# A two-layer graph and expert network on one core: row additions leave GpSimd, norms share instructions, and the last sixteen batches start three expert pairs in a period

## The chip, the cores and the metric

The kernel runs on one core of a Trainium2 chip. The metric is the device time of one execution in microseconds. Before the change it is 1796.04 us, the median of three runs (1791.09, 1796.04 and 1798.93 us). A difference of about 0.5% is the least that such runs can tell from no change.

The core has five engines with a queue of instructions each: TensorE (PE in the profile, its weight loads apart as PEld), VectorE (DVE), ScalarE (ACT), GpSimd (POOL) and SyncE (SP), which here only starts transfers. An engine works through its own queue in order, so an instruction that waits holds up all that stand behind it.

## The reference

64 batches of 256 rows by 256 columns pass two layers. All batches share one 256 x 256 neighbour matrix. What counts for this change is the number of norms (four for each batch), the two residual additions, and the routing of each row to two of eight experts:

```python
# layer 0 (adj_ffn)
x = x + _L0_gnn_ref(_layernorm(x, axis=-1), adj, L0_gnn_W, L0_gnn_a)   # 4 heads, softmax over neighbours, ELU
x = x + _L0_ffn_ref(_layernorm(x, axis=-1), L0_ffn_weight, L0_ffn_bias)  # x @ W.T + bias
# layer 1 (adj_ffn)
x = x + _L1_gnn_ref(_layernorm(x, axis=-1), adj, L1_gnn_W, L1_gnn_a)   # 1 head, ReLU
x = x + _L1_ffn_ref(_layernorm(x, axis=-1), router_w, w1, b1, w2, b2)

def _moe(tokens, router_w, w1, b1, w2, b2):      # the last of the four
    probs = softmax(tokens @ router_w.T)
    rw, re = top_k(probs, 2)                     # two experts for each row
    rw = rw / rw.sum(-1)
    out = tokens
    for e in range(8):
        h = gelu(tokens @ w1[e] + b1[e])
        out = out + combine[:, e:e+1] * (h @ w2[e] + b2[e])
```

## The kernel before

**Tiles and jobs.** A batch is a tile of 128 partitions x 2 x 256 numbers. The program is unrolled in Python. Every batch is a generator (`batch_layers`, from line 373) that emits some instructions, yields a rank, and goes on when it is next called. The loop at the end of the kernel function (lines 895 to 925) counts steps. In a step each live generator is called once, in the order of its last rank, lowest first, so the order of instructions on every engine is written by this loop and not by a planner. Three steps are a period (`TICKS = 3`), and a new batch begins in the first step of each period (phase 0). A batch lives for about 18 steps, so six batches are in work at once, three steps apart.

**The norms.** `norm_stats` (line 287) lets VectorE gather mean and variance (`bn_stats`, `bn_aggr`, lines 290 and 291), and GpSimd then makes 1/sqrt(variance + eps) in two instructions, an addition (line 293) and a power (line 294), over two numbers for each partition. A batch has four norms. By the order of the steps, the norm of one batch's input and that of another's first residual fall in phase 0 of every period; the norm before layer 1's attention and the one before the experts, again of two different batches, fall in phase 1. `rstd`, the result, is first used a step or more later: as the scale in ScalarE's exponentials (line 323) and VectorE's product (line 327) of `projected`, in VectorE's residual (line 414), and in `by` (lines 440 and 443).

**The two additions.** GpSimd adds the bias row to the first residual (`x1b`, line 401, in phase 0) and the ReLU result to the second (`x2`, line 434, in phase 0). Both work on 128 x 512 numbers.

**The experts.** Batches are routed in chunks: twelve of 4 batches, six of 2 and two of 1. The last two batches (`dense`) run through all eight experts instead. After a chunk's routing on VectorE (`top_two`, `route`, `allot`), GpSimd sends every row to its two places in a table in DRAM (`send`, line 741: 16 indirect transfers for a chunk of 4 batches). A send is emitted two at a time, in the steps of phase 1 and 2 only: `later` (line 752) yields again in phase 0. A pair of tiles (256 rows of one expert) is the unit of expert work (`expert_pair`): SyncE loads the pair (`xr`, line 599), the next step loads the expert's weights (`we`, line 610), the next transposes on TensorE (`px`, line 617), the next does the first product (`ph`, line 649), and after that come the second (`py`, line 664), VectorE's bias addition into `y` (line 670), ScalarE's scaling of `y` (line 642), and at last `scatter` (line 681), in which GpSimd starts two indirect transfers that add the 256 rows to the output. The rows of two pairs may meet, so the transfers of a pair wait for both of the pair before. One pair is scattered in a step.

**How pairs begin.** In phase 2 of each period a credit grows by 2 (by 3 when no batch is left to begin) up to 3, and each waiting pair that begins takes 1:

```python
if phase == 2:
    credit = min(credit + (2.0 if more else 3.0), 3.0)
    while waiting and credit >= 1.0:
        credit -= 1.0
        begin(waiting.pop(0)(), 90)
```

A chunk of 4 batches brings 8 pairs at once, so with an empty list behind it the credit has grown to 3, and four periods begin 3, 2, 2 and 1 pairs. 131 pairs are begun in all, 14 of them at the very end for the partly filled tiles. There are six buffers for `y`, five for `xr`, seven for `we`. The two dense batches bring 16 further jobs of the same kind, without sends and scatters, two in a period at the end; their results take `y` buffers too. The output of the last dense batch is stored behind the last scatter.

Of the kernel before, what the change touches and what calls it, by code (L numbers as in the profile page):

```python
# [26 lines left out]
def kernel(  # L27
# [17 lines left out]
    nc = tc.nc  # L45
    B, N, D = x.shape
# [4 lines left out]
    NT = N // P  # L51
    EPS = 1e-5
# [6 lines left out]
    CHUNKS = (4,) * 12 + (2,) * 6 + (1, 1)  # L59
# [9 lines left out]
    TICKS = 3  # L69

    const = ctx.enter_context(tc.tile_pool(name="const", bufs=1))
    io = ctx.enter_context(tc.tile_pool(name="io", bufs=2))
    work = ctx.enter_context(tc.tile_pool(name="work", bufs=2))
# [33 lines left out]
    nc.vector.memset(ones, 1.0)  # L107
    mean_w = const.tile([P, P], F32, tag="mean_w", name="mean_w")
    nc.vector.memset(mean_w, 1.0 / D)
    mhalf = const.tile([P, NT], F32, tag="mhalf", name="mhalf")  # L110
    nc.vector.memset(mhalf, -0.5)

    adj_i = work.tile([P, NT, N], adj.dtype, tag="z", name="adj_i", bufs=6)
# [25 lines left out]
    def gnn_weights(w, a, heads, slope, name):  # L139

        d = D // heads
        wx = const.tile([P, KT, heads, d + 3], F32, tag=name, name=name)
        for k in range(KT):
            nc.sync.dma_start(
                out=wx[:, k, :, :d],  # L150
                in_=w[k * P : (k + 1) * P, :].rearrange("p (h d) -> p h d", h=heads),
            )
        av = work.tile([P, 2, d], F32, tag="e", name=name + "_a")
        nc.scalar.dma_start(out=av.rearrange("p s d -> p (s d)"), in_=rows_to_all(a, 2 * d))
        prod = work.tile([P, heads, d], F32, tag="hp", name=name + "_p")
        for k in range(KT):
            for s, c in ((0, d + 1), (1, d)):
                nc.vector.tensor_mul(
                    prod, wx[:, k, :, :d], av[:, s : s + 1, :].to_broadcast([P, heads, d])
                )  # L160
                nc.vector.tensor_reduce(wx[:, k, :, c : c + 1], prod, AX.X, ALU.add)
            nc.vector.tensor_scalar(
                wx[:, k, :, d + 1 : d + 2], wx[:, k, :, d + 1 : d + 2], 1.0 - slope, None,
                op0=ALU.mult,
            )
            nc.vector.tensor_scalar(
                wx[:, k, :, d + 2 : d + 3], wx[:, k, :, d : d + 1], slope - 1.0, None,
                op0=ALU.mult,
            )
        flat = wx.rearrange("p k h c -> p k (h c)")  # L170
        center(flat, heads * (d + 3))
        return flat
# [29 lines left out]


    C_B1, WROW = KT * D, KT * D + 64
    WBUFS, XBUFS = 7, 5
    wpack = tc.dram_tile([E, P, WROW], F32, name="wpack")
    w2s = const.tile([P, E, KT * D], F32, tag="w2s", name="w2s")
    b2s = const.tile([P, E, D], F32, tag="b2s", name="b2s")
# [74 lines left out]

    def norm_stats(src):
        stats = small.tile([P, NT, 6], F32, tag="stats", name="stats")
        mv = small.tile([P, NT, 2], F32, tag="mv", name="mv", bufs=6)
        for t in range(NT):
            nc.vector.bn_stats(stats[:, t, :], src[:, t, :])  # L290
            nc.vector.bn_aggr(mv[:, t, :], stats[:, t, :])  # L291
        rstd = small.tile([P, NT], F32, tag="rstd", name="rstd", bufs=8)
        nc.gpsimd.tensor_scalar_add(rstd, mv[:, :, 1], EPS)  # L293
        nc.gpsimd.tensor_tensor(rstd, rstd, mhalf, ALU.pow)  # L294
        return mv, rstd

    def transposed(src, tag="xT", bufs=4):
        pt = bank("pt", [KT, N])
# [71 lines left out]
    def batch_layers(b, c0, xng, lg):  # L370
# [4 lines left out]
        _, rstd = norm_stats(x0)  # L375
# [14 lines left out]
                rinv[:, t, :, None].to_broadcast([P, H, HD]), ALU.mult,  # L390
            )
        yield 20
        ex = work.tile([P, NT, D], F32, tag="e", name="e")
        nc.scalar.activation(ex, hp, AF.Exp)

        x1 = work.tile([P, NT, D], F32, tag="x1", name="x1", bufs=2)
        nc.vector.scalar_tensor_tensor(x1, hp, 0.0, x0, op0=ALU.max, op1=ALU.add)
        nc.vector.scalar_tensor_tensor(x1, ex, 1.0, x1, op0=ALU.min, op1=ALU.add)
        yield 30
        x1b = work.tile([P, NT, D], F32, tag="x1b", name="x1b")  # L400
        nc.gpsimd.tensor_add(x1b, x1, bias_f[:, None, :].to_broadcast([P, NT, D]))
        _, rstd = norm_stats(x1)
        xT = transposed(x1)
        yield 70
# [25 lines left out]
        for t, pv in enumerate(pvs):  # L430
            nc.scalar.activation(  # L431
                rel[:, t, :], pv[:, 0, :D], AF.Relu, scale=rinv[:, t, :]
            )
        nc.gpsimd.tensor_add(x2, x2, rel)  # L434
        yield 60
        mv, rstd = norm_stats(x2)
        yield 15

# [221 lines left out]
    def result(hT, e):  # L660
        py = bank("py", [2, D])
        for t in range(2):
            for f in range(KT):
                nc.tensor.matmul(  # L664
                    py[:, t, :], hT[:, f, t * P : (t + 1) * P],
                    w2s[:, e, f * D : (f + 1) * D].rearrange("p e c -> p (e c)"),
                    start=(f == 0), stop=(f == KT - 1),
                )
        y = io.tile([P, 2, D], F32, tag="y", name="y", bufs=6)
        nc.vector.tensor_add(y, py, b2s[:, e, :].to_broadcast([P, 2, D]))  # L670
        return y

# [76 lines left out]
        sent.append(d.ins.name)  # L749
        nc.gpsimd.nop()  # L750

    def later(rank):

        yield rank
        while (len(order_steps) - 1) % TICKS == 0:
            yield rank

    def route(c, row0, nt, n, last, xng, lg):
# [3 lines left out]
        ohs, first, ed = top_two(c, nt, lg)  # L762
        m = rt([E, nt], "m")
        tt(m.rearrange("p e t -> p t e"), ohs[0], ohs[1], ALU.add)
        yield from later(75)

        mf = m.rearrange("p e t -> p (e t)")
        pp = bank("pp", [2, E, nt])
# [26 lines left out]
            vec.tensor_reduce(posf[:, k], ohs[k], AX.X, ALU.add)  # L795
        pos = rt([2, nt], "pos", 4, I32)
        vec.tensor_copy(pos, posf)
        yield from later(75)
        r4 = rt([nt, 4], "r4")
        vec.tensor_scalar(r4[:, :, 0:1], token[:, :nt, None], float(row0), None, op0=ALU.add)  # L800
        vec.tensor_scalar(r4[:, :, 1:2], first[:, :, None], float(E), None, op0=ALU.add)
# [7 lines left out]
        if last:  # L809
            tt(at, at, run[:, :, nt - 1], ALU.add)  # L810
            ends_at = rt([E], "ends_at", 2, I32)
            vec.tensor_copy(ends_at, at)
        yield from later(95)
        mark = len(sent)
        for t in range(nt):
            for k in range(2):
                send(xng[t // NT][:, t % NT, :], pos[:, k, t : t + 1])
            if not last:
                yield from later(95)
            elif t % 2:  # L820
                yield 95
        needs = sent[mark:]
# [72 lines left out]
    batches = jobs()  # L895
    step, more, credit = 0, True, 0.0
    SETUP_AT = 4
    with tc.manual_schedule():
        while more or active or waiting or dense_jobs or scatters:
            phase = step % TICKS  # L900
            if phase == 0 and more:
                nxt = next(batches, None)
                more = nxt is not None
                if more:
                    begin(nxt, 40)
            if step >= SETUP_AT and setup:
                begin(setup.pop(0)(), 90)
            if phase == 2:
                credit = min(credit + (2.0 if more else 3.0), 3.0)
                while waiting and credit >= 1.0:  # L910
                    credit -= 1.0
                    begin(waiting.pop(0)(), 90)
                for _ in range(2):
                    if dense_jobs:
                        begin(dense_jobs.pop(0)(), 90)
            if scatters:
                def one():
                    scatter()
                    return
                    yield  # L920
                begin(one(), 97)
            order_steps.append(step)
            for entry in sorted(active, key=lambda a: a[:2]):
                entry[0] = next(entry[2], None)
            active[:] = [a for a in active if a[0] is not None]
            step += 1

# [34 lines left out]
```

## Time and profile before

| | us |
|---|---|
| median of three runs | 1796.04 |
| the profiled execution's own time | 1822.89 |
| its span, from the first instruction to the last | 1821.2 |
| TensorE matmuls busy | 1629.5 (89%) |
| TensorE weight loads busy | 1433.0 (79%) |
| VectorE busy | 1231.4 (68%) |
| GpSimd busy | 1084.2 (60%) |
| ScalarE busy | 839.9 (46%) |
| mean granted TensorE clock | 0.937 of full speed |

The profiled execution is 1.5% longer than the median of the runs. Durations are its own. The page gives for each engine the busy time and its share of the span, then the span in 40 slices, then groups of instructions by line, with the mean of one and the idle time before them. Other views list who waited for whom, instructions in order of time, and the busy times in a stretch. Weight loads overlap matmuls, so the two rows of TensorE are not to be added. An indirect transfer's busy time on GpSimd is that of making its descriptors, not of the transfer.

### The profile page before, as it was taken

The page shows a single profiled execution, that of the slowest core. Times are in us where ns is not written, and L with a number is a line of the kernel's source. Part 1 is how long each engine was busy: PE and PEld are TensorE (multiplying, and loading weights), DVE is VectorE, ACT ScalarE, POOL GpSimd, SP SyncE. Part 2 cuts the span into 40 slices and gives each one's busy share as a digit, 9 for nine tenths or more (in the row PEclk, how much of TensorE's full clock was granted, in tenths as well). Part 3 has the DMA queues.
Part 4 walks back from the last instruction along what each step waited for, and adds up shares of the span by engine and source line. Part 5 has one row for each costly group of instructions (what it writes and reads, how often), then busy time and mean ns, then how long its engine had stood idle before and what let it go on. Part 6 is the DMA issues. An engine that isn't in the chain of part 4 may idle for free. (4 is left out here: it accounts for less than half of the span.)

```text
span 1821.2 us, 30155 instructions
## 1 busy us (share of the span) xinstructions
PE 1629.5 (89%) x9254; PEld 1433.0 (79%) x9254; DVE 1231.4 (68%) x4680; ACT 839.9 (46%) x1773; POOL 1084.2 (60%) x1164
## 2 busy tenths in 40 slices
PE   6998889899999999999999999999989998778692
PEld 5787778788888888888878788887878887667582
DVE  6889887867685858686766768688678876522231
ACT  1243333355554555554545545555455545443241
POOL 1333645557575767767676757576685767644444
PEclk9999989899998999998989999999899989889897
DMA  4410211235344444544354534444353436576663
GB/s 137 140 36 24 71 60 53 79 109 121 105 95 104 109 126 108 132 103 110 93 119 112 119 91 95 118 111 128 84 127 101 107 82 166 118 186 139 135 139 43
DMA packets 137374, 192.90 MB, mean 106 GB/s; under 512 B 18680, under 2 KB 91392, under 8 KB 137216
## 3 DMA queue, kind: packets, MB, share of 16 engines
q1 hardware_dynamic: 86592, 122.61, 22.0%
q0 software_dynamic: 49632, 67.39, 20.6%
q8 instruction: 76, 1.25, 0.3%
q10 hardware_dynamic: 992, 0.99, 0.2%
q14 instruction: 82, 0.67, 0.1%
HBM read 101.77 MB, written 89.15 MB: 105 GB/s over the span
## 5 line engine op out<-in xcount | busy, mean ns | idle before, releaser
L681 POOL DMA_INDIRECT out_dram<-y,to x262 | 419.4, 1601 | 231.1 <-DMA out_dram<-y,to 103.5
L360 PE MATMUL pv<-q,z 128*128 128x65 f32 (+1 forms) x2560 | 394.4, 314 | 5.3 <-DVE z L346 5.0
L360 PEld LDWEIGHTS pv<-q,z 128*128 128x128 f32 x2560 | 364.9, 210 | 21.1 <-DVE z L346 5.4
L293 POOL TENSOR_SCALAR rstd<-mv 128x2 f32<-128x2 f32 x256 | 81.2, 317 | 376.2 <-DVE mv L291 355.6
L741 POOL DMA_INDIRECT xs<-xng,pos x248 | 261.2, 1053 | 68.2 <-issue 66.0
L315 PE MATMUL pq<-wx,xT 128*128 128x268 f32 (+1 forms) x1024 | 265.4, 402 | 35.8 <-ACT xT L305 31.8
L649 PE MATMUL ph<-sT,we 128*128 128x256 f32 x1048 | 252.6, 397 | 48.1 <-ACT sT L621 22.9
L346 DVE SCALAR_TENSOR_TENSOR z<-pd,q,mask 128x256 f32<-128x256 f32 x640 | 265.1, 473 | 9.9 <-PE pd L339 7.5
L649 PEld LDWEIGHTS ph<-sT,we 128*128 128x128 f32 x1048 | 205.0, 200 | 80.6 <-ACT sT L621 29.4
L664 PE MATMUL py<-w2s,hT 128*128 (+1 forms) x1176 | 265.4, 381 | 0.6 <-ACT hT L655 0.6
L315 PEld LDWEIGHTS pq<-wx,xT 128*128 128x128 f32 x1024 | 188.1, 194 | 85.8 <-ACT xT L305 50.6
L664 PEld LDWEIGHTS py<-w2s,hT 128*128 128x128 f32 x1176 | 220.5, 191 | 29.3 <-ACT hT L655 1.0
L305 ACT COPY xT<-pt 128x512 f32<-128x512 f32 x256 | 144.9, 589 | 192.8 <-PE pt L301 127.6
L327 DVE SCALAR_TENSOR_TENSOR q<-pq,rstd,q 128x256 f32<-128x256 f32 x256 | 112.4, 479 | 154.5 <-ACT q L323 150.7
L655 ACT ACTIVATE hT<-ph,we 128x256 f32<-128x256 f32 x294 | 123.3, 471 | 173.4 <-PE ph L649 122.9
L670 DVE TENSOR_TENSOR y<-py,b2s 128x512 f32<-128x512 f32 x147 | 96.7, 688 | 149.2 <-PE py L664 77.9
L294 POOL TENSOR_TENSOR rstd<-rstd,mhalf 128x2 f32<-128x2 f32 x256 | 184.2, 719 | 21.4
L642 ACT ACTIVATE y<-y,w 128x256 f32<-128x256 f32 x262 | 112.9, 498 | 177.5 <-DVE y L670 171.1
L290 DVE BATCH_NORM_STATS2 stats<-x 128x6 f32<-128x256 f32 x384 | 155.9, 406 | 0.0
L408 PE MATMUL pf<-wfT,xT 128*128 128x256 f32 x512 | 145.7, 435 | 0.1
L323 ACT ACTIVATE q<-pq,rstd 128x12 f32<-128x12 f32 (+1 forms) x256 | 56.5, 265 | 162.3 <-POOL rstd L294 150.8
L434 POOL TENSOR_TENSOR x<-x,rel 128x512 f32<-128x512 f32 x64 | 109.2, 1706 | 25.2 <-ACT rel L431 25.0
(147 smaller groups left out, 2259.2 us busy)
## 6 DMA issues: line engine op xcount, KB each, us to landing
we<-wpack SPq DMA_DIRECT2D x147, 288.0 KB
xr<-xs SPq DMA_DIRECT2D x131, 260.0 KB
xin<-in_x_dram SPq DMA_DIRECT2D x64, 256.0 KB
out_dram<-base SPq DMA_DIRECT2D x64, 256.0 KB
out_dram<-y,to POOLq DMA_INDIRECT x262
xs<-xng,pos POOLq DMA_INDIRECT x248
xs<-fill SPq DMA_DIRECT2D x9, 260.0 KB
wpack<-wt SPq DMA_DIRECT2D x8, 288.0 KB
```

The lines of the kernel that those rows point to most:

```text
L290: nc.vector.bn_stats(stats[:, t, :], src[:, t, :])
L294: nc.gpsimd.tensor_tensor(rstd, rstd, mhalf, ALU.pow)
L305: nc.scalar.copy(dst, pt)
L315: nc.tensor.matmul(pq.rearrange("p h c -> p (h c)"), xT[:, k, t * P : (t + 1) * P], wx[:, k, :], start=(k == 0), stop=(k == KT - 1),)
L346: nc.vector.scalar_tensor_tensor(z[:, j, :], pd[:, i, :], q[:, j, h, d + 2 : d + 3], mask[:, j, :], op0=ALU.max, op1=ALU.mult,)
L360: nc.tensor.matmul(pv[:, h, :], z[:, j, t * P : (t + 1) * P], q[:, j, h, : d + 1], start=(j == 0), stop=(j == NT - 1),)
L408: nc.tensor.matmul(pf[:, t, :], xT[:, k, t * P : (t + 1) * P], wfT[:, k, :], start=(k == 0), stop=(k == KT - 1),)
L649: nc.tensor.matmul(ph[:, f, :], we[:, k * D + f * P : k * D + (f + 1) * P], xT[:, k, :], start=(k == 0), stop=(k == KT - 1),)
L655: nc.scalar.activation(hT[:, f, :], ph[:, f, :], AF.Gelu, bias=we[:, C_B1 + f : C_B1 + f + 1])
L664: nc.tensor.matmul(py[:, t, :], hT[:, f, t * P : (t + 1) * P], w2s[:, e, f * D : (f + 1) * D].rearrange("p e c -> p (e c)"), start=(f == 0 ...
L681: d = nc.gpsimd.indirect_dma_start(out=out_rows, out_offset=bass.IndirectOffsetOnAxis(ap=to[:, t : t + 1], axis=0), in_=y[:, t, :], in_off ...
L741: d = nc.gpsimd.indirect_dma_start(out=xs_d[: E * CAP * PAIR, :], out_offset=bass.IndirectOffsetOnAxis(ap=at, axis=0), in_=xe, in_offset=None,
```

## The change

GpSimd's two additions go to VectorE: the one for `x1b` stands right after `x1`, a step earlier than before, and the one for `x2` a step later than before, ahead of the statistics that read it. Two norms of a step share one addition and one power over four numbers; when a step has a single norm, the loop finishes it after all other work of that step. From batch 48 on (step 144) the credit grows by 3. The last four routed chunks also send in phase 0. `y` has eight buffers, and the ELU's exponential `e` one instead of two.

```diff
-    mhalf = const.tile([P, NT], F32, tag="mhalf", name="mhalf")
+    mhalf = const.tile([P, 2 * NT], F32, tag="mhalf", name="mhalf")
...
-    WBUFS, XBUFS = 7, 5
+    WBUFS, XBUFS, YBUFS = 7, 5, 8
...
+    half_done = []
+
     def norm_stats(src):
         stats = small.tile([P, NT, 6], F32, tag="stats", name="stats")
-        mv = small.tile([P, NT, 2], F32, tag="mv", name="mv", bufs=6)
+        if half_done:
+            mv, rstd = half_done[0]
+            at = NT
+        else:
+            mv = small.tile([P, 2 * NT, 2], F32, tag="mv", name="mv", bufs=4)
+            rstd = small.tile([P, 2 * NT], F32, tag="rstd", name="rstd", bufs=5)
+            half_done.append((mv, rstd))
+            at = 0
         for t in range(NT):
             nc.vector.bn_stats(stats[:, t, :], src[:, t, :])
-            nc.vector.bn_aggr(mv[:, t, :], stats[:, t, :])
-        rstd = small.tile([P, NT], F32, tag="rstd", name="rstd", bufs=8)
-        nc.gpsimd.tensor_scalar_add(rstd, mv[:, :, 1], EPS)
-        nc.gpsimd.tensor_tensor(rstd, rstd, mhalf, ALU.pow)
-        return mv, rstd
+            nc.vector.bn_aggr(mv[:, at + t, :], stats[:, t, :])
+        if at:
+            finish_norms(2 * NT)
+        return mv[:, at : at + NT, :], rstd[:, at : at + NT]
+
+    def finish_norms(n):
+        mv, rstd = half_done.pop()
+        nc.gpsimd.tensor_scalar_add(rstd[:, :n], mv[:, :n, 1], EPS)
+        nc.gpsimd.tensor_tensor(rstd[:, :n], rstd[:, :n], mhalf[:, :n], ALU.pow)
...
-        ex = work.tile([P, NT, D], F32, tag="e", name="e")
+        ex = work.tile([P, NT, D], F32, tag="e", name="e", bufs=1)
...
+        x1b = work.tile([P, NT, D], F32, tag="x1b", name="x1b")
+        nc.vector.tensor_add(x1b, x1, bias_f[:, None, :].to_broadcast([P, NT, D]))
         yield 30
-        x1b = work.tile([P, NT, D], F32, tag="x1b", name="x1b")
-        nc.gpsimd.tensor_add(x1b, x1, bias_f[:, None, :].to_broadcast([P, NT, D]))
         _, rstd = norm_stats(x1)
...
-        nc.gpsimd.tensor_add(x2, x2, rel)
         yield 60
+        nc.vector.tensor_add(x2, x2, rel)
         mv, rstd = norm_stats(x2)
...
-        y = io.tile([P, 2, D], F32, tag="y", name="y", bufs=6)
+        y = io.tile([P, 2, D], F32, tag="y", name="y", bufs=YBUFS)
...
-    def later(rank):
+    def later(rank, c):
         yield rank
-        while (len(order_steps) - 1) % TICKS == 0:
+        while (len(order_steps) - 1) % TICKS == 0 and c < len(CHUNKS) - 4:
             yield rank
...
+    DRAIN_AT = TICKS * (B - 16)
...
-                credit = min(credit + (2.0 if more else 3.0), 3.0)
+                credit = min(credit + (2.0 if step < DRAIN_AT else 3.0), 3.0)
...
             for entry in sorted(active, key=lambda a: a[:2]):
                 entry[0] = next(entry[2], None)
+            if half_done:
+                finish_norms(NT)
```

More of the change, by code (lines that the diff above doesn't have):

```diff
@@ L152, in gnn_weights @@
             )
-        av = work.tile([P, 2, d], F32, tag="e", name=name + "_a")
+        av = work.tile([P, 2, d], F32, tag="e", name=name + "_a", bufs=1)
         nc.scalar.dma_start(out=av.rearrange("p s d -> p (s d)"), in_=rows_to_all(a, 2 * d))
@@ L764, in route @@
         tt(m.rearrange("p e t -> p t e"), ohs[0], ohs[1], ALU.add)
-        yield from later(75)
+        yield from later(75, c)
         mf = m.rearrange("p e t -> p (e t)")
@@ L797, in route @@
         vec.tensor_copy(pos, posf)
-        yield from later(75)
+        yield from later(75, c)
         r4 = rt([nt, 4], "r4")
@@ L812, in route @@
             vec.tensor_copy(ends_at, at)
-        yield from later(95)
+        yield from later(95, c)
         mark = len(sent)
@@ L818, in route @@
             if not last:
-                yield from later(95)
+                yield from later(95, c)
             elif t % 2:
```

## The prediction

> **What bounds the kernel now.** I read the page first, then the busy times by stretch, the instructions around one stall, and the end.
>
> ```profile
> PE 1629.5 (89%) x9254; PEld 1433.0 (79%) x9254; DVE 1231.4 (68%) x4680; ACT 839.9 (46%) x1773; POOL 1084.2 (60%) x1164
> PEclk9999989899998999998989999999899989889897
> ```
>
> TensorE is nearly full, but its clock falls again and again (granted 0.937 on average). To see why, I cut the middle into periods, from one batch's first transpose to the next. A chunk of four batches repeats periods of about 24.4, 23.0, 21.3 and 31 us. The long one is the period in which three pairs were begun at once. Two of these, with busy time and count of PE, PEld, DVE, ACT and POOL in turn, then clock, DMA share and GB/s:
>
> ```profile
> 739.50:765.40 25.90, 23.39 (x144) 20.52 (x143) 15.89 (x55) 14.65 (x29) 20.76 (x22) 1.00 0.64 160
> 834.10:865.10 31.00, 28.29 (x144) 25.07 (x143) 16.05 (x55) 14.66 (x29) 21.36 (x22) 0.83 0.55 143
> ```
>
> The same 144 matmuls take 25.9 us at full clock and 31.0 us at 0.83: half speed for some 10 us. What precedes it shows at 450 us in the order of time, here on POOL, ACT, DVE, POOL, SP and PE in turn:
>
> ```profile
> 427.18 1.84 POOL L401 TENSOR_TENSOR x1b<-x,bias_f 128x512 f32<-128x512 f32 x1
> 428.42 0.79 POOL L293 TENSOR_SCALAR rstd<-mv 128x2 f32<-128x2 f32 x1
> ...
> 430.30 0.71 POOL L294 TENSOR_TENSOR rstd<-rstd,mhalf 128x2 f32<-128x2 f32 x1
> 431.04 0.43 ACT L323 ACTIVATE q<-pq,rstd 128x12 f32<-128x12 f32 x2 [1.63 <-POOL rstd L294]
> 431.35 0.88 DVE L327 SCALAR_TENSOR_TENSOR q<-pq,rstd,q 128x256 f32<-128x256 f32 x2 [2.30 <-ACT q L323]
> ...
> 436.50 0.22 POOL L293 TENSOR_SCALAR rstd<-mv 128x2 f32<-128x2 f32 x1 [0.75 <-DVE mv L291]
> ...
> 439.09 1.26 POOL L741 DMA_INDIRECT xs<-xng,pos  x1 [0.30 <-issue]
> 442.73 2.93 SPq L599 DMA_DIRECT2D xr<-xs  x3
> 448.85 0.63 PE L617 MATMUL px<-ident,xr 128*128 128x128 f32 x4 [1.88 <-DMA xr<-xs]
> 449.31 6.28 PE L360 MATMUL pv<-q,z 128*128 128x65 f32 x32
> ```
>
> This is one chain. GpSimd finishes a scatter at 426.49, then does two additions and two norms until 431.0; ScalarE waits for the second norm, VectorE waits for ScalarE, and from there VectorE runs without a pause to the statistics of phase 1, behind which stand that phase's norm and two sends. SyncE's load of pairs waits for the send before it (545.2 us of such waits in its own view, 33 of them). With two pairs the data are in time; with three the third is 1.88 us late, the clock falls to 0.5 from 450.0 to 460.3, and the next 32 matmuls take 6.28 us where 3.80 us is usual.
>
> At the end TensorE is no longer the bound:
>
> ```profile
> 1804.95 1.55 POOL L681 DMA_INDIRECT out_dram<-y,to  x1 [3.04 <-DMA out_dram<-y,to]
> 1806.81 1.55 POOL L681 DMA_INDIRECT out_dram<-y,to  x1 [0.30 <-issue]
> 1811.22 1.55 POOL L681 DMA_INDIRECT out_dram<-y,to  x1 [2.86 <-DMA out_dram<-y,to]
> ```
>
> Each pair's scatter waits for the one before to land, at least some 6.4 us from pair to pair (1804.95 to 1811.22 is 6.27). The last 29 pairs start from 1615.70 to 1811.22, 6.98 us each.
>
> **The change part by part**, against the profiled execution of 1822.9 us (span 1821.2); the runs' median is 0.985 of it, and the result is scaled by that.
>
> *Additions and norms.* GpSimd loses two additions of 1.70 us a batch (109.2 and 108.1 us in 64). In a stall's chain they take 2.5 us, since they overlap a little. Four norms of 0.317 + 0.719 us become two. A power over four numbers is not in the trace; it lies between 0.71 us (two numbers cost no more than the fixed part) and 1.22 us (the 0.5 us by which power exceeds the addition's 0.21 us is all per number). I take 1.0, the middle, as no row is nearer. At 450 us the shared norm then starts when the last statistics are in, 426.94, and ends at 428.3 instead of 431.0. VectorE's 2.30 us wait goes, as its work before it (line 346) ends at 429.05. VectorE gains two additions of 0.69 us (line 398 does 128x512 with both inputs in SBUF in 0.692). The one for x2 lies in this very chain, ahead of the statistics, and costs 0.69; the one for x1b lies in phase 2, in idle time before the next waits. The longer power costs the sends 0.3. Sends and loads move forward by 2.3 - 0.7 - 0.3 = 1.3 us. The scatter in between starts no earlier than its predecessor's landing (about 429.4), and at its 3.5 us ends before the new norm. The stall of 1.88 us shrinks to about 0.6, and the other seven chunks look alike (VectorE waits 2.65 to 4.06 us at this place, TensorE 1.46 to 2.5).
>
> Here a rule and a row differ. "TensorE: Matmul & The Clock Gate" of the Trainium skill (Part 1) has the clock fall after an idle window of about 3.4 us. By it no gap here is long enough, and eight stalls are worth 8 x 1.3 = 10 us. In this trace gaps of 1.82 to 2.5 us were followed by 6.8 or 10.2 us at half clock seven times out of seven, and one of 1.46 us was not. I go by the rows. The seven long periods exceed 25.9 us by 5.0, 4.8, 4.0, 5.1, 5.5, 5.9 and 3.6 us, 33.9 together; with the 10 of the stalls that is 44, and I take **-40**, one chunk keeping its stall. Between the ends: 0 if the loads come no earlier, -50 if the stalls vanish.
>
> A second rule speaks against moving the additions. "SBUF — State Buffer" (Who interferes with whom) says that a VectorE instruction with two SBUF inputs shuts out a GpSimd instruction that reads SBUF. The trace agrees: the norm's addition takes 0.21 us, or 0.79 at 428.42. By the rule 128 moved additions could each hold GpSimd for 0.6 us, 77 us in all. But the one for x2 precedes the statistics that its norm waits for, and that for x1b meets sends; I count nothing, and 0.6 us on the path wherever they do meet.
>
> *VectorE's own limit.* Around 1251 to 1276 and 1355 to 1390 us, where two-batch chunks are routed, VectorE hardly pauses. There its 1.38 us a period has no cover: six such periods, **+8**. GpSimd waits for it there up to 9.4 us, and TensorE behind that.
>
> *Single norms* occur at the start and for the last batches; then the norm stands behind that step's scatter (up to 4 us of waiting for its predecessor). What is late is VectorE's residual or `by` in the next step. For some four norms with half of it on the path: **+4** (0 to 16).
>
> *Three pairs a period.* Following the loop step by step, the last scatter comes four steps sooner (237 steps become 233), and by step 208, when the last batches end, 107 pairs are scattered instead of 102. Five pairs move into the full part. On TensorE a pair is 1.87 + 1.78 + 0.44 us (a third of `ph` x24 5.60 and of `py` x24 5.34, and `px` x4): 4.1 us, so **+20** if TensorE is full there, +5 if they fall into the pauses of 5.6 and 6.3 us around 1551 and 1573. I take 20. Each brings its loads on SyncE's queue (260 and 288 KB) and two scatters of 1.85 us each on GpSimd, which has just been relieved of more. Seven more periods start with three loads; if two keep a stall long enough for the clock, at 5 us each, **+10** (0 to 42).
>
> *The tail.* Five pairs fewer: 5 x 6.98 = **-35**. Eight `y` buffers: VectorE waited for one 10 times, 48.5 us in all, and behind it a store and weight loads queued on SyncE, until TensorE stood for 15 us at 1692. The 28 steps of 6.98 us are 16 us over 6.4; half of that, **-8** (0 to -16). `e` with one buffer: its next writing comes a period after its reading, nothing. Sends in phase 0 let the last chunks' pairs wait in the list sooner, where five already wait: nothing.
>
> Sum: -40 + 8 + 4 + 20 + 10 - 35 - 8 = -41, so 1782 us, and times 0.985 **1755 us**.
>
> **The rivals.**
>
> (1) *The loads come no earlier*, since another wait (a scatter, the added VectorE work, the longer power) takes the place of the rstd wait, or the plain runs, 27 us faster than the profiled one, have few half-clock stretches to lose. Then the first term is 0: -1 us, **1795 us**. For it: GpSimd idles 0.75 us ahead of phase 1's norm, so it is not itself what is short there. Against it: VectorE's wait for rstd stands in all eight chains.
>
> (2) *Slower: the third load is late in every period.* If stalls stay and each of the seven added three-load periods gets one, the terms are 0 and +42: 0 + 8 + 4 + 20 + 42 - 35 - 8 = +31, **1826 us**. It decides from a third load about 1.5 us late on, the longest gap that left the clock alone. For it: VectorE is fuller in this stretch. Against it: the same relief acts there.
>
> (3) *More gain*: the five pairs fill pauses (+5), no added stall, full relief in the tail: -40 + 8 + 4 + 5 + 0 - 35 - 16 = -74, **1722 us**.
>
> **How the numbers follow.** Forecast 0.56, rival 1 0.16, rival 2 0.10, rival 3 0.18. The forecast alone spans 1738 to 1778. For 8 in 10 the range reaches over rival 1 and most of rival 3: 1715 to 1799. The measurement can tell about 0.5%, 9 us: rival 1 gives most of its chance to "within", a little to either side. Faster 0.80, same 0.10, slower 0.10.
>
> **What would show it.** Right: VectorE's wait before line 327 (2.3 us and more) gone; third transposes under 1 us late; three-pair periods of 25 to 26 us and clock slices without the regular dips; 24 instead of 29 pairs in the tail at 6.4 to 7 us. Wrong: half-clock stretches after 1070 us more frequent than before; GpSimd's norms waiting longer for VectorE's statistics; pairs in the tail at 7 us or more in spite of the buffers.

## The result, and the profile after

After the change the kernel takes 1766.45 us (median of four runs, 1762.49 to 1771.64), against 1793.64 us for the kernel before (four runs, 1791.09 to 1798.93): a ratio of 0.985, 95% interval 0.981 to 0.989. It is faster by 27 us. The forecast of 1755 us is 11 us, or 0.6%, too low; its direction and range held.

The profiled execution after took 1769.78 us (span 1768.1). That is 53 us below the profiled execution before, twice what the runs show, because the one profiled before had lost the clock more often than most (it stood 1.5% above its median). A second profile of the kernel before, span 1801.2 us, is therefore used beside the first.

Page of the kernel after, busy times and granted clock in 40 slices:

```profile
PE 1594.2 (90%) x9254; PEld 1401.9 (79%) x9254; DVE 1297.7 (73%) x4808; ACT 827.5 (47%) x1767; POOL 840.5 (48%) x788
PEclk9999899999999999899999999898998999898997
```

GpSimd has lost 244 us of busy time and VectorE has gained 66. The same 9254 matmuls are busy 35 us less. Of the first 25 slices of the clock two are at 8 tenths, against five in before's first profile; from slice 26 on the dips remain.

Windows of the kernel after, two of the periods in which three pairs begin (busy time and count of PE, PEld, DVE, ACT and POOL, then clock, DMA share and GB/s):

```profile
541.70:566.50 24.80, 23.31 (x144) 20.56 (x143) 18.01 (x59) 15.29 (x31) 16.63 (x15) 1.00 0.62 162
728.30:759.70 31.40, 28.66 (x145) 25.14 (x144) 18.38 (x59) 15.57 (x31) 17.42 (x16) 0.84 0.54 139
```

Between batches 20 and 48 seven such periods take 24.3 to 24.8 us, but for one of 31.3 us. In the first profile of before they take 25.9 to 31.8, in the second 25.2 to 32.8; the sums are 212, 201 and 179 us. This is the chain of the prediction in the kernel after, in order of time, at the same chunk (DVE, POOL, SP, PE, ACT and DVE in turn):

```profile
438.47 0.88 DVE L341 SCALAR_TENSOR_TENSOR q<-pq,rstd,q 128x256 f32<-128x256 f32 x2 [0.55 <-ACT q L337]
440.54 0.68 DVE L449 TENSOR_TENSOR x<-x,rel 128x512 f32<-128x512 f32 x1
444.35 0.23 POOL L308 TENSOR_SCALAR rstd<-mv 128x4 f32<-128x4 f32 x1 [1.70 <-DVE mv L301]
444.67 1.04 POOL L309 TENSOR_TENSOR rstd<-rstd,mhalf 128x4 f32<-128x4 f32 x1
447.31 0.98 POOL L755 DMA_INDIRECT xs<-xng,pos  x1 [0.30 <-issue]
450.29 1.50 SPq L613 DMA_DIRECT2D xr<-xs  x3
455.51 0.63 PE L631 MATMUL px<-ident,xr 128*128 128x128 f32 x4 [0.28 <-DMA xr<-xs]
```

VectorE's wait of 2.30 us is 0.55 us, the third transpose is 0.28 us late instead of 1.88, and the clock holds.

The end, GpSimd in the kernel after:

```profile
1751.20 1.56 POOL L695 DMA_INDIRECT out_dram<-y,to  x1 [2.79 <-DMA out_dram<-y,to]
1753.07 1.56 POOL L695 DMA_INDIRECT out_dram<-y,to  x1 [0.30 <-issue]
1757.66 1.56 POOL L695 DMA_INDIRECT out_dram<-y,to  x1 [3.03 <-DMA out_dram<-y,to]
```

Still one landing after another. The last 24 pairs start 7.02 us apart, against 6.99 before.

Where the time lies, worked out from the traces: us from the span's start to batch 4, then between the first transposes of batches 4, 20, 48 and 63, and from there to the end; in brackets the us at half clock.

| kernel | to 4 | 4 to 20 | 20 to 48 | 48 to 63 | to the end |
|---|---|---|---|---|---|
| before, first profile | 65.9 | 305.9 | 694.9 (58.0) | 383.2 (30.7) | 371.3 |
| before, second profile | 68.1 | 303.8 | 683.2 (41.0) | 375.7 (23.9) | 370.5 |
| after | 69.9 | 309.6 | 661.5 (13.7) | 389.4 (34.1) | 337.7 |
| additions and norms only | 69.1 | 305.9 | 666.0 (20.5) | 360.8 (6.8) | 366.6 |
| additions only | 72.1 | 305.0 | 661.4 (17.1) | 369.3 (20.5) | 360.4 |
| shared norms only | 70.0 | 307.3 | 689.3 (54.6) | 385.6 (41.0) | 364.8 |
| fillers for the additions | 70.4 | 310.2 | 679.7 (20.5) | 376.8 (20.5) | 367.8 |
| end only | 72.2 | 306.6 | 671.4 (20.5) | 399.5 (37.5) | 340.2 |
| additions and end, single norms | 72.3 | 306.3 | 671.1 (20.5) | 386.6 (17.1) | 334.5 |

The last six rows belong to experiments below. Against the second profile of before, the middle gains 22 us, batches 48 to 63 lose 14, the end gains 33. One profile of a stage is not its size, though: the kernel with the end's edits only, which between batches 20 and 48 differs from before in the number of `y` and `e` buffers alone, took 671.4 us there, 12 less than before's second profile. How the 27 us divide is therefore read from the medians of the runs below.

### The profile page after: what moved, and what is told of

The parts are those of the page before. It is cut to its first block, busy times and chain, and to the rows that moved or that the text cites. A ratio compares the mean times of both kernels' runs of the same rounds, so it can differ in the third digit from the quotient of the medians.

```text
span 1768.1 us, 29994 instructions
## 1 busy us (share of the span) xinstructions
PE 1594.2 (90%) x9254; PEld 1401.9 (79%) x9254; DVE 1297.7 (73%) x4808; ACT 827.5 (47%) x1767; POOL 840.5 (48%) x788
## 5 line engine op out<-in xcount | busy, mean ns | idle before, releaser
L374 PE MATMUL pv<-q,z 128*128 128x65 f32 (+1 forms) x2560 | 370.9, 301 | 4.4 <-DVE y L684 4.4
L374 PEld LDWEIGHTS pv<-q,z 128*128 128x128 f32 x2560 | 342.0, 198 | 18.9 <-DVE y L684 5.4
L308 POOL TENSOR_SCALAR rstd<-mv 128x4 f32<-128x4 f32 (+1 forms) x132 | 45.2, 342 | 543.5 <-DVE mv L301 475.8
L329 PE MATMUL pq<-wx,xT 128*128 128x268 f32 (+1 forms) x1024 | 270.4, 409 | 36.6 <-ACT xT L319 36.6
L755 POOL DMA_INDIRECT xs<-xng,pos x248 | 251.9, 1016 | 69.2 <-issue 66.9
L663 PE MATMUL ph<-sT,we 128*128 128x256 f32 x1048 | 243.3, 388 | 27.7 <-ACT sT L635 19.5
L309 POOL TENSOR_TENSOR rstd<-rstd,mhalf 128x4 f32<-128x4 f32 (+1 forms) x132 | 135.6, 1027 | 10.9
L422 PE MATMUL pf<-wfT,xT 128*128 128x256 f32 x512 | 131.9, 403 | 2.6 <-ACT xT L319 2.6
L353 PE MATMUL pd<-ident,q 128*128 128x128 f32 x640 | 104.9, 279 | 13.7 <-ACT q L337 12.3
L408 ACT ACTIVATE e<-hp 128x512 f32<-128x512 f32 x64 | 40.3, 630 | 164.2 <-DVE hp L402 164.2
```

Source lines behind the costliest of these rows:

```text
L309: nc.gpsimd.tensor_tensor(rstd[:, :n], rstd[:, :n], mhalf[:, :n], ALU.pow)
L329: nc.tensor.matmul(pq.rearrange("p h c -> p (h c)"), xT[:, k, t * P : (t + 1) * P], wx[:, k, :], start=(k == 0), stop=(k == KT - 1),)
L374: nc.tensor.matmul(pv[:, h, :], z[:, j, t * P : (t + 1) * P], q[:, j, h, : d + 1], start=(j == 0), stop=(j == NT - 1),)
L422: nc.tensor.matmul(pf[:, t, :], xT[:, k, t * P : (t + 1) * P], wfT[:, k, :], start=(k == 0), stop=(k == KT - 1),)
L663: nc.tensor.matmul(ph[:, f, :], we[:, k * D + f * P : k * D + (f + 1) * P], xT[:, k, :], start=(k == 0), stop=(k == KT - 1),)
L755: d = nc.gpsimd.indirect_dma_start(out=xs_d[: E * CAP * PAIR, :], out_offset=bass.IndirectOffsetOnAxis(ap=at, axis=0), in_=xe, in_offset=None,
```

## The experiments

Ratios are to runs of the kernel before on the same chip, with 95% intervals. The reasons to be tested: that relieving GpSimd brings the loads forward (the forecast), against the loads coming no earlier and the gain being the end's.

**The kernel before, profiled again**, unchanged.

> The kernel before, unchanged, for a second profile. The profiled execution of before took 1822.9 us while its median is 1794 us. Theory A (the half-clock stretches behind late third loads belong to every execution): this profile shows the same dips, about one in each chunk of four batches between 340 and 1150 us, and the 27 us lie elsewhere. Theory B (they belong to the disturbed execution): a profile near 1795 us shows three-pair periods of 25 to 26 us and at most two of the seven dips.

1793.70 us, ratio 1.002 (0.999 to 1.004). Four of its seven three-pair periods between batches 20 and 48 took 29 us or more, three took 25.2. So the loss by the clock is real and usual, and smaller than the first profile had it: against an undisturbed 24.5 us, the seven periods hold 29 us too much, not 40.

**Additions and shared norms only** (`credit`, the sends and the six `y` buffers as before), and **the end only** (three pairs from batch 48 on, sends in phase 0, eight `y` buffers; the additions on GpSimd, each norm by itself). `e` has one buffer in these two and in all runs below but the next; the norms-only run, which has it too, shows no gain from it.

> Only GpSimd's relief: both additions on VectorE and the norms shared; credit, sends and six y buffers as before. Theory A (the second norm's lateness makes the third load late and the clock fall): no half-clock stretch between 340 and 1060 us but one or two, three-pair periods of 24.5 us, and 20 to 30 us less than before. Theory B (the gain is the tail's): within 5 us of before. Theory C (VectorE's 1.4 us a period weigh as much as the relief): 5 to 15 us slower.

> Only the end: three pairs in a period from batch 48 on, the last four chunks sending in every step, eight y buffers and one e buffer; GpSimd keeps its additions and single norms. Theory A (each three-pair period without the relief has a late third load): -34 us in the tail, +20 for the five pairs that move, and up to seven added stalls of 5 us, so -14 to +20 us, near no change. Theory B (the tail makes the gain): 25 to 30 us less than before, all that the whole change gives.

The first: 1769.91 us, 0.988 (0.983 to 0.992). The second: 1783.01 us, 0.995 (0.993 to 0.998). The relief gives about 22 us and the end about 9. The two together, which is the change, give 0.985, not distinct from the relief by itself.

**Two pairs a period at most**, so that no third load exists until the batches are out:

```diff
-                credit = min(credit + (2.0 if more else 3.0), 3.0)
+                credit = min(credit + (2.0 if more else 3.0), 2.0 if more else 3.0)
```

> The kernel before with the credit held at 2 until no batch is left to begin, so no period of the full part loads three pairs; nothing else differs. One step more in all (238). Theory A (the third load is what comes late): no gap over 1 us ahead of the transposes of pairs and no regular half-clock stretch between 340 and 1150 us, 25 us less there, 7 us more at the end: 10 to 25 us less than before. Theory B (the clock falls for another reason): the dips stay and the time is 0 to 10 us more.

1822.33 us, 1.017 (1.012 to 1.023): slower, where a gain was expected. The chunk's eight pairs now take four full periods, and the fourth meets the next chunk's routing on VectorE. The waits of TensorE at that place, with VectorE's and GpSimd's instructions ahead of them, in time order:

```profile
520.20 3.73 DVE L564 TENSOR_SCALAR ef<-ef 128x8 f32<-128x8 f32 x1
520.80 1.87 POOL L434 TENSOR_TENSOR x<-x,rel 128x512 f32<-128x512 f32 x1
522.03 1.86 POOL L401 TENSOR_TENSOR x1b<-x,bias_f 128x512 f32<-128x512 f32 x1
527.27 0.63 PE L301 MATMUL pt<-ident,xng 128*128 128x128 f32 x4 [2.17 <-DVE z L346]
530.82 2.45 PE L360 MATMUL pv<-q,z 128*128 128x65 f32 x20 [2.05 <-DVE y L670]
```

Two gaps of about 2 us appear in every one of these chunks, in a period that takes 27.2 to 33.2 us between batches 20 and 48; in the one shown it is 30.6 us, with VectorE busy 22.73. One stands behind a VectorE instruction on eight numbers that lasts 3.73 us and ends with GpSimd's second addition. Two causes offer themselves: that hold, or VectorE having no room. A later run takes the hold away.

**The additions only** (single norms), against **the shared norms only** (additions on GpSimd):

```diff
+        nc.vector.tensor_add(x1b, x1, bias_f[:, None, :].to_broadcast([P, NT, D]))
         yield 30
-        nc.gpsimd.tensor_add(x1b, x1, bias_f[:, None, :].to_broadcast([P, NT, D]))
...
-        nc.gpsimd.tensor_add(x2, x2, rel)
         yield 60
+        nc.vector.tensor_add(x2, x2, rel)
```

> Only the two additions move to VectorE; norms stay single, and the end is as before. Seen by now: in every run whose GpSimd does the additions, some of VectorE's small instructions last up to 3.9 us and end within 0.1 us of an addition of GpSimd; in the two runs without them none does. Theory L (VectorE is held by these additions, and the chain is shorter without them): no such held instruction, 15 to 22 us less than before, most of what the relief gives. Theory N (the late norm is what counts, whoever is in front of it): additions are 2.5 of some 3.6 us of the chain less 0.7 us on VectorE, so 8 to 15 us.

> Only the norms share instructions; GpSimd keeps its additions. The chain to the third load is about 1.1 us shorter, and nothing is added to VectorE. Theory N (chain length decides): third loads 1 us less late, fewer half-clock stretches, 10 to 15 us less than before. Theory L: VectorE is still held by additions (about 20 us in all in an execution), 0 to 6 us less than before.

The additions: 1765.49 us, 0.982 (0.978 to 0.986), a gain of 33 us (25 to 40), more than either reason had given them. The norms: 1813.12 us, 1.005 (1.002 to 1.008), where both reasons had expected no loss. The whole gain is the additions'; the norms bring none and may cost a little. The groups of VectorE's product with `rstd`, with the idle time ahead of it and what ended most of that, for before (second profile):

```profile
L327 DVE SCALAR_TENSOR_TENSOR q<-pq,rstd,q 128x256 f32<-128x256 f32 x256 | 112.7, 478 | 154.5 <-ACT q L323 154.4
```

for the norms only:

```profile
L341 DVE SCALAR_TENSOR_TENSOR q<-pq,rstd,q 128x256 f32<-128x256 f32 x256 | 112.1, 479 | 141.2 <-ACT q L337 132.0
```

and for the additions only:

```profile
L327 DVE SCALAR_TENSOR_TENSOR q<-pq,rstd,q 128x256 f32<-128x256 f32 x256 | 112.1, 478 | 77.4 <-ACT q L323 75.9
```

The wait that the prediction named is halved by the additions and hardly touched by the norms. GpSimd in one chunk of the norms-only kernel shows why:

```profile
432.88 1.88 POOL L448 TENSOR_TENSOR x<-x,rel 128x512 f32<-128x512 f32 x1
434.11 1.87 POOL L415 TENSOR_TENSOR x1b<-x,bias_f 128x512 f32<-128x512 f32 x1
435.36 0.82 POOL L308 TENSOR_SCALAR rstd<-mv 128x4 f32<-128x4 f32 x1
436.26 1.04 POOL L309 TENSOR_TENSOR rstd<-rstd,mhalf 128x4 f32<-128x4 f32 x1
```

The additions hold GpSimd for 2.48 us (432.88 to 435.36) before the norm, whether it is one norm or two. The shared norm then takes 1.94 us (435.36 to 437.30), two single ones in the prediction's chunk 2.59 (428.42 to 431.01): 0.6 us saved. That is given back in part by the norm just ahead of the sends: its power takes 1.04 us over four numbers against 0.72 over two. VectorE still waits 2.95 us at 437.64 there, and the third transpose is 2.68 us late.

**Fillers for the additions.** The additions are on VectorE, and GpSimd fills an unused tile in their old places, so that its time ahead of the norms is about what it was (3.01 us in the chunk shown, against 2.48 of the additions). The result is computed as before, the fills are extra work.

```diff
+        nc.vector.tensor_add(x1b, x1, bias_f[:, None, :].to_broadcast([P, NT, D]))
         yield 30
-        nc.gpsimd.tensor_add(x1b, x1, bias_f[:, None, :].to_broadcast([P, NT, D]))
+        nc.gpsimd.memset(busy, 0.0)
+        nc.gpsimd.memset(busy[:, :384], 0.0)
...
-        nc.gpsimd.tensor_add(x2, x2, rel)
+        nc.gpsimd.memset(busy, 0.0)
         yield 60
+        nc.vector.tensor_add(x2, x2, rel)
```

> The additions alone on VectorE (1765 us), and in the two places where GpSimd had them it now fills an unused tile (1024, then 1024 and 384 numbers for each partition), which takes some 2.5 us and reads nothing. Theory Q (what the additions cost is GpSimd's time ahead of the norms in phase 0): third loads late again with gaps of 1.5 us and more, three-pair periods of 25 to 32 us, and 20 to 35 us more than the additions alone, so 1785 to 1800 us. Theory L (what they cost is that VectorE's instructions are held): no held instruction, and within 8 us of 1765 us.

1808.83 us, 1.003 (1.001 to 1.006): the gain is gone. The fills ahead of the norm on GpSimd, in one chunk:

```profile
436.37 1.54 POOL L437 MEMSET busy<- 128x1024 f32 x1
437.97 0.95 POOL L403 MEMSET busy<- 128x1024 f32 x1
438.98 0.42 POOL L404 MEMSET busy<- 128x384 f32 x1
439.38 0.22 POOL L294 TENSOR_SCALAR rstd<-mv 128x2 f32<-128x2 f32 x1
```

VectorE's product waits again:

```profile
L328 DVE SCALAR_TENSOR_TENSOR q<-pq,rstd,q 128x256 f32<-128x256 f32 x256 | 112.3, 478 | 139.1 <-ACT q L324 134.7
```

So what the additions cost was GpSimd's time ahead of the norm, and not where the sums were computed. The size is not exact, since the fills hold GpSimd 0.5 us longer than the additions did and VectorE keeps its added work. Nor does all fit: this kernel's third transposes are 0.2 to 1.7 us late, against 0.7 to 2.7 in the second profile of before, and it has half as much half clock between batches 20 and 48 (20.5 us against 41.0) at nearly the same length of that stage. Here the time is lost more by waiting and less by the clock.

**Two pairs at most, with additions and norms moved.**

> The credit held at 2 as in the run that took 28 us more, now with both additions on VectorE and shared norms. There one instruction of the pair allotment on VectorE lasted 3.5 us instead of 0.17 in nearly each chunk, and ended with GpSimd's second addition. Theory L: that instruction is back at 0.17 us, no stall of 2 us before the transposes of the routed rows, and the time is within 8 us of the relief alone (1770 us). Rival (VectorE has no room for two pairs in the period that also allots, held or not: 23.2 us busy of 22.6 to 30): the stall stays and the time is over 1795 us.

1816.76 us, 1.011 (1.006 to 1.016). The same place, in time order:

```profile
522.12 0.17 DVE L578 TENSOR_SCALAR ef<-ef 128x8 f32<-128x8 f32 x1
525.63 0.63 PE L315 MATMUL pt<-ident,xng 128*128 128x128 f32 x4 [0.19 <-DVE z L360]
529.18 4.11 PE L374 MATMUL pv<-q,z 128*128 128x65 f32 x18 [2.05 <-DVE y L684]
```

The held instruction and its gap of 2.17 us are gone, the gap of 2.05 us behind `y` is not, and the period is 30.2 us at a clock of 0.83 with VectorE busy 22.07 us. So both causes were there: the hold, which the moved additions take away, and the wait for VectorE's `y`, which they don't. That wait stands in all seven chunks between batches 20 and 48. In six of them 6.8 or 10.2 us at half clock follow and the period takes 28.5 to 30.3 us; in the seventh the clock holds and it takes 25.7. In that stage the lost clock accounts for what this run is behind the kernel after: 51.2 us at half speed against 13.7, which is 19 us of work, and the stage is 19 us longer. With the credit of 3 the period holds one pair. That VectorE has no room for two there is argued from its busy time and was not tested.

**Six `y` buffers in the kernel after.**

> The changed kernel with six y buffers instead of eight. Forecast's term: 8 us more than the changed kernel (1774 us), in the tail, where VectorE waits for a buffer. Rival: the buffers are worth nothing, since the scatter chain takes 6.4 to 7 us a pair in either case: within 3 us of 1766 us.

1774.49 us, 0.987 (0.982 to 0.991): 8 us above after in the medians, 4 by the ratios; the intervals overlap. The rate at the end is the same (6.97 us a pair over the last 24), and VectorE's additions into `y` wait 54.7 us for a buffer instead of 38.8. The end begins later: the last norm starts at 1561.5 us instead of 1550.8.

**Additions with parts of the end**: with the whole end, norms single; with eight `y` buffers and nothing else of the end; and with the whole end, but the third pair begun a step later from batch 48 on:

```diff
-                while waiting and credit >= 1.0:
+                begun = 0
+                while waiting and credit >= 1.0 and (begun < 2 or step < DRAIN_AT):
+                    begun += 1
                     credit -= 1.0
                     begin(waiting.pop(0)(), 90)
+            if phase == 0 and step > DRAIN_AT and waiting and credit >= 1.0:
+                credit -= 1.0
+                begin(waiting.pop(0)(), 90)
```

> The changed kernel without its shared norms: additions on VectorE, three pairs a period at the end, sends in every step for the last chunks, eight y buffers. If sharing is worth nothing or costs a little (norms alone: 0.5% over before), this is 0 to 8 us under the changed kernel, 1758 to 1766 us. If sharing helps once the additions are gone, 5 us or more over it.

> The additions on VectorE and eight y buffers; credit and sends as before. Six buffers cost the changed kernel 8 us. If the buffers work alone: 1757 us, 8 under the additions alone. If they work only with the three pairs a period: 1763 to 1768 us. Against the run with the end's other edits this shows what those are worth; theory: five pairs leave the tail (-35) and cost as much in the full part, so within 5 us of each other.

> As the run with additions and end, but from batch 48 on the third pair of a period begins one step later (phase 0) than the first two. Theory (the added three-pair periods lose the clock through their third load): half-clock time between batches 48 and 63 falls from some 34 us to under 15, and 8 to 14 us less than with three at once. Rival (VectorE is too full there, whatever the loads): within 4 us of it.

They take 1770.59 us, 0.982 (0.976 to 0.987); 1769.20 us, 0.983 (0.977 to 0.988); and 1780.37 us, 0.987 (0.982 to 0.993). Beside the additions neither the end's edits nor the buffers show a gain, and spreading the third pair brings none: batches 48 to 63 take 394.5 us with it, 23.9 of them at half clock, against 386.6 and 17.1 without. So it is not shown that a third load begun at once is what this stage pays for. None of these is shown to be faster than the kernel after.

## Why the prediction was right, and where its sizes were off

**Additions and norms (-40, +8, +4).** The mechanism held in the main: the wait for `rstd` delays a chain that ends in the third load, and with a late load the clock falls. With the additions on GpSimd (before twice, norms only, end only) 17 of 28 three-pair periods between batches 20 and 48 took 28 us or more, each with a stretch at half clock; with the additions on VectorE (seven kernels) 8 of 49 did. It is a matter of frequency and not of every chunk: in the end-only profile, where the product waits as long as in before,

```profile
L327 DVE SCALAR_TENSOR_TENSOR q<-pq,rstd,q 128x256 f32<-128x256 f32 x256 | 112.6, 478 | 163.6 <-ACT q L323 163.3
```

five of the seven third transposes came 0.4 to 1.2 us late and the clock held. What made those loads earlier is open. The sum of the three terms was -28, and the two edits by themselves measured -22 (14 to 30, from the interval). Inside the sum three things were off.
- The step "the shared norm ends at 428.3 instead of 431.0" credited both edits together with 2.7 us. All of it that counts is the additions'. I had worked out the norm's saving and the longer power's cost separately and not asked what each edit would give without the other; norms alone gave nothing.
- The size -40 came from one execution, in which seven of eight chunks lost the clock. Between batches 20 and 48 the stage shortened by 33 us against that profile and by 22 against the second one. Scaling by 0.985 did not correct for this, since what differed between the two executions of before was mostly this very term (11.7 of the 20 us between their spans).
- The +8 for VectorE was put at the two-batch chunks. Those gained (stage 48 to 63: 375.7 to 360.8 us with the relief alone). The loss appeared where I had costed none: from batch 4 to 12, before any pair exists, the kernel before took 134.8 us and the relief alone 143.5. It comes with the additions and not with the norms: 143.8 us with the additions only, 137.2 with the norms only. I read it as VectorE's 1.4 us a period with no other work to cover it; no run tests that.

Against the rule on the clock the rows were right: between batches 20 and 48 alone the stage gave back more than the 10 us of the late transposes, 22 us against before's second profile.

On the second rule, counting nothing for the moved additions was right, but the row that was to show the rule does not. At 428.42 the norm's addition begins while GpSimd's own addition before it still runs, until 429.02; 42 such places in before's first profile take 0.75 us on average, and the 22 in which that addition had ended take 0.22. One row does fit (GpSimd, then VectorE):

```profile
1493.93 0.70 POOL L293 TENSOR_SCALAR rstd<-mv 128x2 f32<-128x2 f32 x1 [2.05 <-DVE mv L291]
1493.88 0.69 DVE L397 SCALAR_TENSOR_TENSOR x<-hp,xin 128x512 f32<-128x512 f32 x1
```

The norm's addition takes 0.70 us here with nothing of GpSimd's ahead of it, as long as VectorE's instruction with two SBUF inputs. It is the only such case in that profile, and the additions-only kernel has one as well.

**Five pairs moved, seven more periods with three loads (+20, +10).** The cost is 29 us, from the relief alone to the kernel after between batches 48 and 63, against 30 predicted; that the two agree is partly luck, as the parts are not settled. In this pair of profiles the clock has about half of it: 34.1 us at half speed instead of 6.8, which is 14 us of work. In the pair with single norms the stage grows by 17 us (369.3 to 386.6) and the clock has no part in it (20.5 us at half speed, then 17.1). At full clock the periods with three pairs take 25.2 to 26.9 us in the kernel after, those with two 23.0 to 24.5 with the relief alone. One part of the cost is a wait of which the prediction had the pieces and did not join them. GpSimd, ScalarE, VectorE and TensorE of the kernel after:

```profile
1223.16 1.60 POOL L695 DMA_INDIRECT out_dram<-y,to  x1 [3.01 <-DMA out_dram<-y,to]
1225.07 1.55 POOL L695 DMA_INDIRECT out_dram<-y,to  x1 [0.30 <-issue]
1226.10 0.80 POOL L308 TENSOR_SCALAR rstd<-mv 128x4 f32<-128x4 f32 x1
1226.98 1.04 POOL L309 TENSOR_TENSOR rstd<-rstd,mhalf 128x4 f32<-128x4 f32 x1
1228.06 0.43 ACT L337 ACTIVATE q<-pq,rstd 128x12 f32<-128x12 f32 x2 [10.26 <-POOL rstd L309]
1228.38 0.58 ACT L319 COPY xT<-pt 128x512 f32<-128x512 f32 x1
1228.36 0.88 DVE L341 SCALAR_TENSOR_TENSOR q<-pq,rstd,q 128x256 f32<-128x256 f32 x2 [6.59 <-ACT q L337]
1229.02 1.22 PE L422 MATMUL pf<-wfT,xT 128*128 128x256 f32 x2 [2.57 <-ACT xT L319]
```

The scatter waits for the one before it to land and the norm stands behind it on GpSimd, though its statistics were ready at 1221.0. ScalarE waits for the norm, VectorE 6.59 us for ScalarE, and TensorE 2.57 us for the copy `xT` that stands behind ScalarE's wait. A period with three pairs has three scatters on GpSimd, each bound to its predecessor. I counted the scatters' issue time and not that their waiting keeps the norms back.

**The tail (-35).** The step was right in its count and in its rate: 29 pairs start after the last norm instead of 34 with the relief alone, and a pair takes 7.0 us. From the last norm to the last scatter is 206.9 us instead of 245.6. But the last norm starts at 1550.8 us instead of 1512.7. The 38 us spent ahead of it are those saved behind it. The tail's pairs start 7.02 us apart, which the prediction had named as a sign of being wrong.

**Eight `y` buffers (-8).** Four us by the ratios, eight in the medians, were measured, neither clear of the noise, and not where the step put them: the end's rate did not change. Without the three-pair end they gave nothing to be seen.

The end's edits as a whole were to give -13. By themselves they gave -9 (4 to 13); beside the relieved GpSimd no gain can be told. So the relief gave 22 of 28 us and the end, beside it, some 3 to 6 of 13 (1769.91 to 1766.45 us, or 0.988 to 0.985; within the uncertainty). The larger part of what is missing is the end's, whose two halves cancel.

**The rivals.** *The loads come no earlier* falls with the additions-only run and the fillers. *Slower, by a late load in every period* is there in part: three periods between batches 48 and 63 of the kernel after take 31 us. *More gain* needed the five pairs to fill pauses; they did not.

## What to carry to other kernels

Ask of an engine that is off the path what stands in its queue just ahead of a value that others wait for: taking 2.5 us of additions from there gave this kernel 33 us (25 to 40), while sharing instructions behind them gave nothing. When work is moved from a tail that runs at a fixed rate into a stretch that is nearly full, compare both prices before counting the first: here five pairs at 7.0 us were bought with as much. When one profiled execution stands above its median, first see whether the term that you mean to remove is what sets it apart, and size that term by a second profile.

## What was not expected of the hardware

**GpSimd's additions hold small VectorE instructions.** In every profile with the additions on GpSimd, 13 or more VectorE instructions that usually take about 0.2 us last 0.5 to 3.9 us, and end within 0.1 us of a GpSimd addition's end. In before, first profile (VectorE, then GpSimd):

```profile
1261.22 2.79 DVE L564 TENSOR_SCALAR ef<-ef 128x4 f32<-128x4 f32 x1 [0.55 <-DVE ef L563]
...
1260.90 1.85 POOL L434 TENSOR_TENSOR x<-x,rel 128x512 f32<-128x512 f32 x1
1262.14 1.84 POOL L401 TENSOR_TENSOR x1b<-x,bias_f 128x512 f32<-128x512 f32 x1
```

VectorE's begins 0.3 us after GpSimd's first addition and ends at 1264.01, GpSimd's second at 1263.98. The excess adds up to 24 us in before's first profile, 28 in its second, 27 with the shared norms only and 31 with the end only; where the additions are on VectorE there is none. The Trainium skill, "SBUF — State Buffer" (Who interferes with whom), says that the two engines share one pair of ports, that whoever issues first holds it and that the other is fully blocked. These rows agree. The prediction had used that rule in one direction only, for VectorE shutting GpSimd out. The steady chunks between batches 20 and 48 of before show no such hold, so it is no part of the 22 us there; what it adds to the gain in batches 48 to 63 (7 us of excess in before's second profile) was not measured apart. The fills, which only write, also held some VectorE instructions, for up to 1.9 us; none of them between batches 20 and 48, so the 18 us by which that stage is longer than with the additions only are not theirs.

**The clock doesn't follow the size of a gap.** A gap of 3.00 us in the additions-only run was followed by 6.8 us at half clock, one of 2.74 us with the relief alone by 10.2; two gaps of 2.1 us close together by 6.8 us in some chunks of the two-at-most run and by nothing in the last three; and after gaps of 0.97 and 0.83 us the kernel after lost 10.2 us at 737. TensorE of the additions-only run, then of the kernel after (two lines):

```profile
1017.68 0.63 PE L617 MATMUL px<-ident,xr 128*128 128x128 f32 x4 [3.00 <-DMA xr<-xs]
735.68 0.63 PE L631 MATMUL px<-ident,xr 128*128 128x128 f32 x4 [0.97 <-DMA xr<-xs]
737.14 1.07 PE L631 MATMUL px<-ident,xr 128*128 128x128 f32 x4 [0.83 <-DMA xr<-xs]
```

The 3.4 us window of the Trainium skill's "TensorE: Matmul & The Clock Gate" (Part 1), as a bound on single gaps, does not describe these traces, and neither does the 1.5 us that the prediction took from before. What can be said is how much half clock an execution had in all: 134 to 157 us in the seven kernels with the additions on VectorE, 167 to 231 us in the four profiles with them on GpSimd (the runs with two pairs at most left aside: 207 and 224).

**A power costs more over four numbers than over two.** 0.72 us over two for each partition in before, 1.05 over four in after; the prediction's 1.0, taken between two bounds, was near.
